# A bias copied into PSUM by ScalarE in place of a bias product, and other segment sizes, in a graph convolution kernel

## Chip, cores and metric

The kernel runs on one core of a Trainium2 chip. The metric is device time in microseconds, the median of several runs. A profile is one further execution of the same program, recorded by the hardware profiler.

## The reference

412,500 edges, sorted by their target node, join 12,500 nodes; each node and each filter has 128 features, each edge has 20 attributes.

```python
h    = maximum(layernorm(x), 0) @ W_in2f
Wij  = (ssp(edge_attr @ W_f1 + b_f1) @ W_f2 + b_f2) * edge_weight[:, None]   # ssp = softplus - log 2
x_ij = h[dst] * Wij                          # dst is sorted
agg  = segment_sum(x_ij, src, num_segments=12500)
out  = x + ssp(agg @ W_o1 + b_o1) @ W_o2 + b_o2
```

The rows of h are gathered by the sorted index, and the messages are summed by the unsorted one, so the sum is a scatter.

## The kernel before, in words

Edges are worked on in chunks of 512 (806 chunks; 4 chunks are a group, 202 groups). A chunk is four columns of 128 edges, one edge on each partition. Two things happen at once: messages are made and scattered into tables in DRAM, and tables that are full are read back and summed.

**Making messages.** The function `step(k)` writes out by hand the order of the work, so each engine's queue holds it in this order, whatever is ready first. For chunk k it does, among other things:

- `hidden` (lines 611 to 621), every second step for two chunks: two products `z` (line 616, TensorE), then Abs and Exp on ScalarE (lines 619 and 620). `hidden_log` is the Ln (line 625, in the other step), and `hidden_end` (line 631, VectorE) makes `r`.
- `value(k+1)` (lines 723 to 732): a product of three rows of ones with three bf16 parts of the bias starts the accumulation of `v` in a PSUM bank (line 726, 512 columns), and four fp32 products `r @ W_f2` (line 730) add to it.
- `picked(k+1)` (lines 711 to 721): four products gather the rows of h (line 714), and four ScalarE copies scaled by the edge weight make `hg` (line 719).
- `message(k)` (lines 734 to 757): VectorE multiplies `v` by `hg` into `o` (line 741), and GpSimd issues four indirect DMAs, one for each 128 edges, that scatter the rows of `o` (with the node's place as a 129th number) to slots of a table (line 745).
- `rank` and `rank_end` (lines 642 to 683): two products on a PSUM bank that is kept throughout (lines 687 and 655) and a VectorE maximum (line 660) find the next free slot of each node block. `blocks` and `window` are comparisons on VectorE (lines 636 and 706).

`v` and `picked` share three PSUM banks (tag "v", bufs=3); `o` has four buffers of two chunks each.

**Summing.** The groups are cut into segments, each with a table of its own: `SEGS = (64, 56, 32, 24, 14, 12)`. Each table has T tiles of 128 rows for each of the 98 node blocks, and one more for blocks near the segment's own nodes; T is 12, 11, 7, 5, 3 and 3. When a segment's chunks have been scattered, its table is read back in units of up to six tiles (`Collect.load`, line 783), VectorE compares the places with a row of numbers (line 794), and each tile is one fp32 product into `acc` (line 807), which is added to the sums in SBUF (line 822 or 824). A planner at lines 917 to 932 spreads the units of the first five segments evenly over the steps from nine after the segment's last chunk to step `NCH + 6` (NCH is 806): 5.39 tiles a step from step 265 to 489, 8.16 to step 713, and 8.24 after it. The last segment can only be collected when all its scatters have landed: it is a tail after the loop (lines 970 to 977), in which each four node blocks are finished at once by `finish` (lines 375 to 403: two more products, softplus, and the output). In tiles that is 4156 for all segments, 304 of them in the tail.

At the beginning, `make_h` (lines 299 to 362) computes h, partly beside the first steps.

Of the kernel before, what the change touches and what calls it, by code (L numbers as in the profile page):

```python
# [9 lines left out]
F32 = mybir.dt.float32  # L10
# [3 lines left out]
AF = mybir.ActivationFunctionType  # L14
# [3 lines left out]
P = 128  # L18
TG = 16
CH = 512  # L20
NCHUNK = TG * P // CH
QT = CH // P
SEGS = (64, 56, 32, 24, 14, 12)
RW = P + 1
VIEWS = 16
BG = 8
# [9 lines left out]
def ceil_div(a, b):  # L36
    return -(-a // b)
# [3 lines left out]
def gnn_kernel(  # L41
# [20 lines left out]
    nc = tc.nc  # L62
# [9 lines left out]
    const = ctx.enter_context(tc.tile_pool(name="const", bufs=1))  # L72

    NBLK = NTILE
    NFLAG = 6 * len(SEGS) + 8
    QB = QT * NBLK
    assert sum(SEGS) == NG
    NCH = ceil_div(n_edges, CH)

    class Segment:  # L80
# [4 lines left out]
        def __init__(self, k):  # L85
            self.g0 = sum(SEGS[:k])
            self.c0 = self.g0 * NCHUNK
            self.c1 = min((self.g0 + SEGS[k]) * NCHUNK, NCH)
            own = [c * CH * N // n_edges for c in (self.c0, self.c1)]

            self.b0 = max(0, own[0] - P // 2) // (P * BG) * BG
            self.b1 = min(NBLK, ceil_div(own[1] + P // 2, P * BG) * BG)
            mean = (SEGS[k] * TG * P - (own[1] - own[0])) / QT * P / N
            self.T = int(ceil_div(2 * (2 * mean + 4 * (2 * mean) ** 0.5), P))

            def low(m):
                return max(0, int(m - 5 * m ** 0.5)) // ZR * ZR

            self.low = low(mean)
            self.low_last = low(mean * (N % P or P) / P)  # L100
            self.rows = self.row(NBLK)
            self.table = tc.dram_tile([self.rows, RW], F32, name=f"slots{k}")

            self.views = dram_disjoint_views(self.table[:, :], VIEWS + 1)

            self.clears = []
            self.cleared = self.c0 + (self.c1 - self.c0) // 2 if k == 0 else self.c0
# [70 lines left out]
    def load(ap, shape, name):  # L178
        t = const.tile(shape, F32, name=name)
        nc.sync.dma_start(t, ap)  # L180
        return t
# [10 lines left out]
    wf2 = load(w_f2, [P, P], "wf2")  # L192
    wo1 = load(w_o1, [P, P], "wo1")
    wo2 = load(w_o2, [P, P], "wo2")
    bf1 = load(b_f1[:, None], [P, 1], "bf1")
    bo1 = load(b_o1[:, None], [P, 1], "bo1")
    bf2 = load(b_f2[None, :].to_broadcast([P, P]), [P, P], "bf2")
# [6 lines left out]
    def spread(t, n):  # L204
        return t[:, None, :].to_broadcast([t.shape[0], n, P])
# [24 lines left out]
    ones_b = const.tile([P, P], BF16, name="ones_b")  # L230
# [8 lines left out]
    nbf1 = const.tile([P, 1], F32, name="nbf1")  # L239
    nc.vector.tensor_scalar(nbf1, bf1, -1.0, None, op0=ALU.mult)  # L240

    bf2_p = const.tile([3, P], BF16, name="bf2_p")
    left = const.tile([1, P], F32, name="bf2_left")
    with tc.tile_pool(name="bias_ps", bufs=1, space=PSUM) as bias_ps:
        b12 = bias_ps.tile([1, P], F32, name="b12")
        nc.tensor.matmul(b12, bf1, wf2, start=True, stop=True)
        nc.vector.tensor_add(left, b12, bf2[0:1, :])
    for k in range(3):
        part = const.tile([1, P], BF16, name=f"bf2_{k}")
        nc.vector.tensor_copy(part, left)  # L250
# [7 lines left out]
    sums = tc.dram_tile([SUMT * P, P], F32, name="sums")  # L258
    segs = [Segment(k) for k in range(len(SEGS))]

# [225 lines left out]
    with tc.tile_pool(name="edge", bufs=2) as edge, tc.tile_pool(  # L486
        name="quad", bufs=3
# [44 lines left out]
        class Group:  # L532
# [176 lines left out]
            def picked(self, c, at):  # L709

                ps = psum.tile([P, QT, P], F32, name="picked", tag="v", bufs=3)
                near = self.near.pop(c)
                for i in range(QT):
                    nc.tensor.matmul(ps[:, i, :], at[:, i * P:(i + 1) * P], near,  # L714
                                     start=True, stop=True)
                hg = quad.tile([P, QT, P], F32, name="hg", bufs=2)
                for i in range(QT):
                    j = c * QT + i
                    nc.scalar.activation(hg[:, i, :], ps[:, i, :], AF.Copy,  # L719
                                         scale=self.rcut[:, j:j + 1])  # L720
                return hg

            def value(self, c):

                v = psum.tile([P, QT, P], F32, name="v", bufs=3)
                nc.tensor.matmul(v.rearrange("p t f -> p (t f)"), ones_b[:3, :], spread(bf2_p, QT),  # L726
                                 start=True, stop=False, skip_group_check=True)
                r = self.pair[c // 2 * 2][:, c % 2, :]
                for i in range(QT):
                    nc.tensor.matmul(v[:, i, :], r[:, i * P:(i + 1) * P], wf2,  # L730
                                     start=False, stop=True, skip_group_check=True)
                return v
# [98 lines left out]
        def of(k):  # L831
            return groups[k // NCHUNK], k % NCHUNK

        hgs, ats, vs = {}, {}, {}

        summed = []

        def step(k, units=()):


            def has(j):
                return 0 <= j < NCH

            j = k + LG
            if has(j) and j % NCHUNK == 0:
                groups[j // NCHUNK] = Group(j // NCHUNK)
            if has(k + LW):
                g, c = of(k + LW)
                g.rows(c)
            for c, u in units:  # L850
                c.load(u + AHEAD)

            j = k + LR + 1
            if has(j):
                g, c = of(j)
                if c == 0:
                    g.columns()
                g.blocks(c)
            j = k + LZ - 2
            if has(j) and j % 2 == 0:  # L860
                g, c = of(j)
                g.hidden_end(c)
            if has(k + 2):
                g, c = of(k + 2)
                g.window(c)
                ats[k + 2] = g.pick
            if has(k):
                g, c = of(k)
                g.message(c, vs.pop(k), hgs.pop(k))
            if has(k + 1):  # L870
                g, c = of(k + 1)
                vs[k + 1] = g.value(c)
            if has(k + 1):
                g, c = of(k + 1)
                hgs[k + 1] = g.picked(c, ats.pop(k + 1))
            for c, u in units:
                c.compare(u)
            j = k + LR
            if has(j):
                g, c = of(j)  # L880
                g.rank(c)
            j = k + LZ
            if has(j) and j % 2 == 0:
                g, c = of(j)
                g.hidden(c)
            j = k + LZ - 1
            if has(j) and j % 2 == 0:
                g, c = of(j)
                g.hidden_log(c)
            for c, u in units:  # L890
                if summed:
                    summed[0].add(summed[1])
                summed[:] = c, u
            j = k + LR
            if has(j):
                g, c = of(j)
                g.rank_end(c)
# [18 lines left out]

        at = [seg.c1 + 9 for seg in segs[:-1]]
        work = [sum(seg.tiles(b) for b in range(NBLK)) for seg in segs[:-1]]
        end = NCH + 6
        rate = {}  # L920
        while len(rate) < len(at):
            n = len(at) - len(rate)
# [3 lines left out]
            end = at[j]  # L926
# [22 lines left out]
        with tc.manual_schedule():  # L949
            h = [make_h(q, psum) for q in range(2)]  # L950
            for m in h + h:
                next(m)
            aside = side()
            relative()
            while h:
                for m in list(h):
                    if next(m, 1):
                        h.remove(m)
            for k in range(-LG, max(NCH, max(units) + 1)):
                for seg, d in zeros.get(k, ()):  # L960
                    seg.clears.append(nc.sync.dma_start(*d).ins.name)
                now = units.get(k, ())
                for c, u in now:
                    if u == 0:
                        for i in range(AHEAD):
                            c.load(i)
                step(k, now)
                next(aside, None)
            summed[0].add(summed[1])
# [13 lines left out]
    with tc.If(missed > 0):  # L983
        with tc.tile_pool(name="any_e", bufs=2) as edge, tc.tile_pool(
            name="any_q", bufs=2
# [51 lines left out]
```

## Time and profile before

| | |
|---|---|
| median of 3 runs | 5830.78 us (5822.29 to 5839.35) |
| the profiled execution | 4396.31 us, its span 4394.5 us |
| mean granted TensorE clock in it | 0.855 of full speed |
| busy: TensorE products, VectorE, GpSimd, ScalarE | 3607, 3140, 3115, 2333 us |
| the 16 DMA engines | mean 189 GB/s |

The profiled execution was 1434 us shorter than the median of the timed runs. So durations of single instructions can be read from the profile, and sums over it are to be held against its own time; what the timed runs did otherwise isn't on the page.

In the rows, a group is named by its line, engine and operation; an fp32 product is recorded as two instructions, so the 4156 tiles of line 807 are 8312 rows. The clock column says which part of full speed TensorE was granted. Of an engine's idle time the profile says what ended it.

### The profile page before, as it was taken

The numbers are of one execution on the slowest core, as the hardware profiler recorded it, in microseconds if no ns is written. First come the engines' busy times: TensorE is split into PE (matmuls) and PEld (weight loads), VectorE is DVE, ScalarE is ACT, GpSimd is POOL, SyncE is SP. The second block draws the span as 40 slices with busy tenths as digits, with TensorE's granted clock in tenths as the row PEclk, the third lists the DMA queues.
The fourth block names the chain that finished last, engine by engine and source line by source line (L and its number), as shares of the span: only waits on it lengthen the run. The fifth ranks groups of instructions, "written<-read, shape, count | busy, mean of one in ns | idle before, by whom it ended". The sixth has DMA issues, their size and how long they took to land.

```text
span 4394.5 us, 72656 instructions
## 1 busy us (share of the span) xinstructions
PE 3607.4 (82%) x22558; PEld 2618.3 (60%) x22558; DVE 3140.1 (71%) x6637; ACT 2332.5 (53%) x4685; POOL 3114.6 (71%) x3288
## 2 busy tenths in 40 slices
PE   3767776777777888888788889999899998989877
PEld 2544444444444666666566567777677776767666
DVE  5766666566555776767667678787888878888766
ACT  3655555555555555555555555555555555545424
POOL 2777777677777777777777777777777777777620
PEclk9776666667666898899998899999999999999999
DMA  5766547888765666765876566666666766766666
GB/s 139 192 178 230 174 128 197 223 223 230 183 208 135 177 178 183 238 193 166 257 197 174 150 179 187 194 195 185 189 188 183 199 191 185 193 188 191 172 180 192
DMA packets 498071, 829.10 MB, mean 189 GB/s; under 512 B 170680, under 2 KB 288300, under 8 KB 497676
## 3 DMA queue, kind: packets, MB, share of 16 engines
q1 hardware_dynamic: 378950, 602.34, 51.2%
q0 software_dynamic: 103168, 213.15, 14.7%
q10 hardware_dynamic: 15558, 8.89, 0.7%
q8 instruction: 182, 2.98, 0.3%
q14 instruction: 213, 1.74, 0.1%
HBM read 425.03 MB, written 398.98 MB: 188 GB/s over the span
## 4 chain that ended last, share of the span: by engine, by line


## 5 line engine op out<-in xcount | busy, mean ns | idle before, releaser
L745 POOL DMA_INDIRECT slots<-o,slot x3224 | 3108.4, 964 | 1106.3 <-issue 803.6
L719 ACT ACTIVATE hg<-picked,rcut 128x128 f32<-128x128 f32 x3224 | 920.8, 369 | 1372.0 <-PE picked L714 1323.5
L807 PEld LDWEIGHTS acc<-to,m 128*128 128x128 f32 x8312 | 1078.7, 205 | 353.8 <-issue 187.7
L807 PE MATMUL acc<-to,m 128*128 128x128 f32 x8312 | 1154.6, 294 | 92.3 <-DVE agg L824 47.3
L730 PEld LDWEIGHTS v<-wf,r 128*128 128x128 f32 x6448 | 918.1, 220 | 303.7 <-issue 303.7
L730 PE MATMUL v<-wf,r 128*128 128x128 f32 x6448 | 1088.2, 320 | 0.0
L616 PE MATMUL z<-f,wf 20*128 20x512 f32 x1612 | 524.2, 726 | 217.5 <-DVE r L631 190.9
L794 DVE TENSOR_TENSOR to<-count_ps,m 128x768 f32<-128x768 f32 (+3 forms) x829 | 657.9, 812 | 51.8 <-PE acc L807 27.7
L619 ACT ACTIVATE a<-z,bf 128x1024 f32<-128x1024 f32 x403 | 449.1, 1114 | 426.7 <-PE z L616 426.7
L660 DVE TENSOR_REDUCE top<-free 128x4 f32<-128x392 f32 x806 | 447.2, 555 | 211.7 <-PE free L655 210.4
L631 DVE SCALAR_TENSOR_TENSOR r<-z,nbf,a 128x1024 f32<-128x1024 f32 x403 | 514.6, 1277 | 94.2 <-ACT a L625 92.5
L741 DVE TENSOR_TENSOR o<-v,hg 128x512 f32<-128x512 f32 x806 | 547.2, 679 | 2.8 <-ACT hg L719 2.1
L739 DVE COPY o<-place 128x8 f32<-128x8 f32 x403 | 80.4, 200 | 650.9 <-DMA slots<-o,slot 650.6
L714 PE MATMUL picked<-near,at 96*128 96x128 bf16 x3224 | 356.4, 240 | 218.0 <-DVE o L741 215.7
L625 ACT ACTIVATE a<-a,half 128x1024 f32<-128x1024 f32 x403 | 468.4, 1162 | 0.0
L636 DVE TENSOR_TENSOR inb<-count_ps,blk 128x392 f16<-128x392 f32 x806 | 445.7, 553 | 0.0
L726 PE MATMUL v<-bf_p,ones_b 3*128 3x512 bf16 x806 | 350.1, 434 | 104.1 <-DVE o L741 93.9
L620 ACT ACTIVATE a<-a 128x1024 f32<-128x1024 f32 x403 | 425.9, 1057 | 12.8
L714 PEld LDWEIGHTS <-at 96*128 96x128 bf16 x3224 | 275.7, 109 | 256.2 <-DVE o L741 224.6
L616 PEld LDWEIGHTS z<-f,wf 20*128 20x128 f32 x1612 | 142.4, 206 | 388.9 <-issue 186.3
L687 PE MATMUL free<-inb,rest_of 128*128 128x392 f16 x806 | 303.1, 376 | 55.0 <-DVE top L660 53.8
L706 DVE TENSOR_TENSOR at<-rel,prow 96x512 bf16<-96x512 bf16 x806 | 331.1, 411 | 0.0
(107 smaller groups left out, 1416.2 us busy)
## 6 DMA issues: line engine op xcount, KB each, us to landing
m<-slots SPq DMA_DIRECT2D x371, 387.0 KB
rel<-rel_d SPq DMA_DIRECT2D x202, 384.0 KB
m<-slots SPq DMA_DIRECT2D x172, 322.5 KB
m<-slots SPq DMA_DIRECT2D x212, 258.0 KB
slots<-o,slot POOLq DMA_INDIRECT x3224
slots<-zero SPq DMA_DIRECT2D x24, 2064.0 KB
f<-in_f_t SPq DMA_DIRECT2D x404, 80.0 KB
slots<-zero SPq DMA_DIRECT2D x22, 1032.0 KB
```

The source lines that it names most:

```text
L616: nc.tensor.matmul(z[:, k, :], wf1[rows, :], self.f[rows, :], start=True, stop=True)
L619: nc.scalar.activation(a, z, AF.Abs, bias=bf1)
L625: nc.scalar.activation(a, a, AF.Ln, bias=half, scale=0.5)
L631: nc.vector.scalar_tensor_tensor(r, z, nbf1, a, op0=ALU.max, op1=ALU.add)
L660: nc.vector.tensor_reduce(self.top[:, c * QT:(c + 1) * QT], free_v, axis=mybir.AxisListType.X, op=ALU.max)
L714: nc.tensor.matmul(ps[:, i, :], at[:, i * P:(i + 1) * P], near, start=True, stop=True)
L719: nc.scalar.activation(hg[:, i, :], ps[:, i, :], AF.Copy, scale=self.rcut[:, j:j + 1])
L730: nc.tensor.matmul(v[:, i, :], r[:, i * P:(i + 1) * P], wf2, start=False, stop=True, skip_group_check=True)
L741: nc.vector.tensor_mul(o[:, :, :P], v, hg)
L745: put = nc.gpsimd.indirect_dma_start(out=views[j % VIEWS], out_offset=bass.IndirectOffsetOnAxis(ap=self.slot[:, j:j + 1], axis=0), in_=o[: ...
L794: nc.vector.tensor_tensor(to[:, :n, :], count_ps[:, None, :].to_broadcast([P, n, P]), self.m[u][:, :n, P:].to_broadcast([P, n, P]), op=ALU ...
L807: nc.tensor.matmul(self.acc[b // QT][:, i, :], m[:, j, :P], to[:, j, :], start=t == 0, stop=t == self.seg.tiles(b) - 1)
```

## The change

Two things are changed. The bias row, which is the same for every edge, is laid out over 128 partitions once, in a tile `bf12`. For every chunk from the third on, ScalarE copies it into the PSUM bank of `v` (`bias`), and the four products of `value` add to what they find there; the first two chunks keep the product. The copy for chunk k+2 is queued in step k, behind the four `hg` copies of chunk k+1 and ahead of Abs, Exp or Ln. The `picked` products set their start flag once for a bank and not four times. And the segments are of 64, 56, 36, 24, 14 and 8 groups, with the planner's end at `NCH + 14`; T becomes 12, 11, 7, 5, 3 and 2, which makes 4058 tiles, 206 of them in the tail.

```diff
-SEGS = (64, 56, 32, 24, 14, 12)
+SEGS = (64, 56, 36, 24, 14, 8)
...
+    bf12 = const.tile([P, P], F32, name="bf12")
...
-        b12 = bias_ps.tile([1, P], F32, name="b12")
-        nc.tensor.matmul(b12, bf1, wf2, start=True, stop=True)
-        nc.vector.tensor_add(left, b12, bf2[0:1, :])
+        b12 = bias_ps.tile([P, P], F32, name="b12")
+        nc.tensor.matmul(b12, bf1.to_broadcast([P, P]), wf2, start=True, stop=True)
+        nc.vector.tensor_add(bf12, b12, bf2)
+    nc.vector.tensor_copy(left, bf12[0:1, :])
...
                     nc.tensor.matmul(ps[:, i, :], at[:, i * P:(i + 1) * P], near,
-                                     start=True, stop=True)
+                                     start=i == 0, stop=i == QT - 1, skip_group_check=True)
...
-            def value(self, c):
+            def bias(self, c):
                 v = psum.tile([P, QT, P], F32, name="v", bufs=3)
-                nc.tensor.matmul(v.rearrange("p t f -> p (t f)"), ones_b[:3, :], spread(bf2_p, QT),
-                                 start=True, stop=False, skip_group_check=True)
+                if self.g * NCHUNK + c < 2:
+                    nc.tensor.matmul(v.rearrange("p t f -> p (t f)"), ones_b[:3, :],
+                                     spread(bf2_p, QT), start=True, stop=False,
+                                     skip_group_check=True)
+                else:
+                    nc.scalar.activation(v, spread(bf12, QT), AF.Copy)
+                return v
+
+            def value(self, c, v):
                 r = self.pair[c // 2 * 2][:, c % 2, :]
...
-                vs[k + 1] = g.value(c)
-            if has(k + 1):
-                g, c = of(k + 1)
+                vs[k + 1] = g.value(c, bs.pop(k + 1))
                 hgs[k + 1] = g.picked(c, ats.pop(k + 1))
+            if has(k + 2):
+                g, c = of(k + 2)
+                bs[k + 2] = g.bias(c)
...
-        end = NCH + 6
+        end = NCH + 14
```

## The prediction, as put on record before the result

> **What bounds the kernel now.** I read the groups first, then the engines by stretch with the clock, then GpSimd's queue, then single steps in order of time. In the groups (line, engine, operation, tiles, count | busy us, mean ns | idle before it), these matter:
>
> ```profile
> L745 POOL DMA_INDIRECT slots<-o,slot x3224 | 3108.4, 964 | 1106.3 <-issue 803.6
> L807 PE MATMUL acc<-to,m 128*128 128x128 f32 x8312 | 1154.6, 294 | 92.3 <-DVE agg L824 47.3
> L739 DVE COPY o<-place 128x8 f32<-128x8 f32 x403 | 80.4, 200 | 650.9 <-DMA slots<-o,slot 650.6
> L726 PE MATMUL v<-bf_p,ones_b 3*128 3x512 bf16 x806 | 350.1, 434 | 104.1 <-DVE o L741 93.9
> L822 ACT ACTIVATE agg<-acc 128x512 f32<-128x512 f32 x24 | 14.2, 591 | 3.4 <-PE acc L807 3.4
> ```
>
> The page puts GpSimd at 71% busy and TensorE at 82%, but VectorE waits 650.6 us for scatters to land so that it gets an `o` buffer back: whoever makes messages is ahead of who scatters them. GpSimd's queue, in order of time (start, duration):
>
> ```profile
> 2999.11 0.95 POOL L745 DMA_INDIRECT slots<-o,slot  x1 [0.31 <-DVE to L794]
> 3000.37 0.96 POOL L745 DMA_INDIRECT slots<-o,slot  x1 [0.30 <-issue]
> 3001.63 0.96 POOL L745 DMA_INDIRECT slots<-o,slot  x1 [0.30 <-issue]
> ```
>
> Start to start is 1.26 us, so a chunk of four takes 5.05 us. By stretch (the columns are length; busy us and instructions of PE, weight load, DVE, ACT, POOL; clock; DMA share; GB/s):
>
> ```profile
> 400.00:600.00 200.00, 145.75 (x737) 89.73 (x737) 128.23 (x317) 117.59 (x244) 152.14 (x158) 0.71 0.57 176
> 3000.00:3200.00 200.00, 182.36 (x1316) 142.81 (x1316) 164.08 (x320) 106.56 (x214) 151.83 (x159) 0.96 0.68 189
> 4220.00:4394.00 174.00, 132.88 (x930) 113.92 (x930) 113.62 (x165) 61.78 (x100) 1.28 (x2) 0.96 0.69 198
> ```
>
> 158 or 159 scatters fit in each 200 us, early and late. So the profiled execution is bound by GpSimd: about 84 us before the first scatter, 3224 × 1.265 = 4078, some stalls, and a tail of 174 us add up to its 4394.5 us. But the timed runs take 5830.78 us, 1434 us more, and this page doesn't say why. It has a hint: the granted clock is often 0.50 while TensorE is busy without a gap. From one such place (start, duration):
>
> ```profile
> 1183.55 0.63 PE L714 MATMUL picked<-near,at 96*128 96x128 bf16 x4
> 1183.98 0.53 PE L687 MATMUL free<-inb,rest_of 128*128 128x392 f16 x1
> 1184.30 0.53 PE L655 MATMUL free<-inb,after 128*128 128x392 f16 x1
> 1184.77 2.08 PE L616 MATMUL z<-f,wf 20*128 20x512 f32 x4
> 1186.63 0.63 PE L726 MATMUL v<-bf_p,ones_b 3*128 3x512 bf16 x1
> 1187.19 2.08 PE L730 MATMUL v<-wf,r 128*128 128x128 f32 x8
> 1189.06 0.63 PE L714 MATMUL picked<-near,at 96*128 96x128 bf16 x4
> 1189.49 0.53 PE L687 MATMUL free<-inb,rest_of 128*128 128x392 f16 x1
> 1189.82 0.53 PE L655 MATMUL free<-inb,after 128*128 128x392 f16 x1
> 1190.93 0.58 PE L726 MATMUL v<-bf_p,ones_b 3*128 3x512 bf16 x1 [0.58 <-ACT hg L719]
> ```
>
> The clock there (length, busy us, count, clock, DMA share, GB/s):
>
> ```profile
> 1180.00:1185.00 5.00, 5.00 (x24) 0.50 0.66 149
> ```
>
> From start to start at half clock: bias product 0.53 to 0.56 us, the four products of v 1.87, picked 0.43, the two rank products 0.8, a pair of z 1.87. A step with z is 5.48 us (1181.15, the bias product before the first line shown, to 1186.63) and one without 3.66 of work, 4.57 on average. A tile of line 807 is two instructions like those of v: 1.87 / 4 = 0.47 us. Now suppose that the timed runs have half clock throughout, and TensorE binds wherever a step of it takes over 5.05 us:
>
> - 80 us of start, and 265 steps before any segment is collected: the pair of steps takes 9.78 us with its wait for hg (1181.15 to 1190.93), 4.89 a step, with about 0.25 of make_h 5.14: 1362.
> - 224 steps with 5.39 tiles: 4.57 + 2.52 = 7.09 each: 1588. 224 with 8.16: 8.38 each: 1877. 93 with 8.24: 8.42 each: 783. Six more: 23.
> - Tail: 304 tiles × 0.47 = 142, and 25 times 3.7 for the two output products (two runs of 1.87): 235 in all.
>
> The sum is 5948 us, 2% over the median and with nothing fitted to it. GpSimd's rate would have to become 1.7 us for no reason that the trace shows. I take it that the timed runs are TensorE at about half clock.
>
> **What the Trainium skill says.** "TensorE: Matmul & The Clock Gate", section "Part 1: The HAM clock gate", has two clock states only, half and full, with half as the default; the trace agrees in its plain 0.50 and 1.00. The page also says that some 3.4 us of activity release it. The trace doesn't agree: from 1005 to 1020 us TensorE was 89 to 100% busy at 0.50. That keeps my reading possible, and doesn't prove it. "Perfetto Trace Analysis", section "GPSIMD Engine Instruction", advises start-to-start spacing over recorded spans, hence 1.26 and not 0.96 us. "ScalarE: Activation LUTs", section "What ACT_TABLE_LOAD costs", prices an ACTIVATE with immediate scale and bias at 186 ns + 0.833 ns an element: an estimate of 613 ns for the new copy. The trace's nearest row, L822, took 591 ns. "PSUM — Partial Sum Buffer", section "The four PSUM rules", says that a product without a start flag adds to what ScalarE wrote only where an earlier product left its mark; that is why picked's flags change, which costs nothing: same products.
>
> **The change, part by part.**
>
> - Removed: 804 bias products, 0.53 us each at half clock (0.31 at full: 3000.46 to 3000.77), and their weight loads, which overlap.
> - Added: 804 copies on ScalarE at 0.59 us = 474 us, onto 2333 of busy time. Both ends: 0.37 (an hg copy, a quarter of the size) and 0.72 (L372). ScalarE then has 2807 us of work in over 5400; it doesn't bind.
> - The new wait: v's first product needs the copy, which stands behind the hg of the chunk before it. From picked's end it is ready after about 0.05 + 1.14 (four hg) + 0.59 + 0.1 = 1.9 us. Behind the waiting product in TensorE's queue are picked, the rank products, z and acc; for hg, message and then GpSimd wait. Cover in a step: two rank products 0.8, z 1.87 every second step, and one or two units of acc, 1.9 us (4 tiles) to 2.8 (6 tiles). With a unit the wait is hidden; planned rates give about one unit in every step from step 265. Without a unit or z, 1.1 us show; the old product too waited 0.58 there. Queued behind the copy are Abs, Exp or Ln, 0.6 us later; z's banks and r have a step of slack.
> - Early stage (265 steps): with z 5.48 − 0.53 = 4.95, without it 1.87 + 0.43 + 1.95 = 4.25; 4.6 on average, with make_h 4.85. That is under GpSimd's 5.05: 1338 instead of 1362. So 265 of the savings are cut to 24 us.
> - Later stages, 0.53 less a step, with the new plan: 224 × 6.56 = 1469; 240 steps with 7.62 tiles × 7.60 = 1824; 77 with 8.97 × 8.23 = 634; 14 steps of 4.19 = 59.
> - Tail: 206 tiles × 0.47 + 93 = 189. The segments' part of the saving is 98 tiles × 0.47 = 46 us. Fewer rows are cleared and read back as well, beside other work.
> - Setting up bf12: one larger product and one more small copy, under 1 us before the first scatter, and hidden by the loads.
>
> The sum after is 80 + 1338 + 1469 + 1824 + 634 + 59 + 189 = 5593, so 355 less. Scaled by 5831 / 5948 it is 348: **5830 − 348 = 5482, say 5480 us.** In the profiled execution, where GpSimd binds, the same edit should give only the shorter tail: 98 tiles at 0.25 us (1.0 / 4 at full clock), some 25 us off 4396.
>
> **Rivals.**
>
> - *A: GpSimd binds in the timed runs too*, at some 1.7 us a scatter. For it: it does bind in the profile. Against: no row shows such a rate. Then only the tail gives: 5830 − 25 to 30 = 5803, at the edge of what can be told.
> - *B: the copy is late, and TensorE waits for it (slower).* Place: ScalarE's queue, where picked may end while Abs and Exp (2.2 us) still run. Then the copy comes after 4.1 us, and a step with rank and one small unit (2.5 of cover) waits 1.6; in half the steps that is 0.8 a step against 0.53 saved. Over 541 steps +146, less 46 for the tiles: 5930. It decides from a mean wait of about 0.6 us a step. Against it: ScalarE is 53% busy and waits 1323.5 us for picked.
> - *C: the clock state isn't a property of the runs but of the kernel*, and the new order falls into full clock: 4396 − 25 = 4370.
>
> **Chances and range.** Forecast 0.60 (own range 5390 to 5570: no early saving, or waits of 0.15 a step, at one end; the unscaled sum and a copy of 0.37 at the other), A 0.18, B 0.17, C 0.05. The range 5390 to 5860 takes in the forecast, A and the near end of B. Faster by over 0.3% (what a measurement here can tell): 0.60 + 0.12 of A + 0.05; same 0.06; slower 0.17.
>
> **What would show it.** The timed median falls by some 6% while the profiled execution falls by under 1%. Line 726 is left with two products; a copy of 128x512 at about 0.6 us appears 804 times; v's first product waits for ScalarE mostly before the first collection. If the profile still shows 158 scatters in 200 us and the median hardly moves, A is right; if v waits for the copy in stretches with acc, B is. The forecast is wrong at its root if a timed run isn't at half clock.

## The result, and the profile after

The changed kernel took **5878.36 us** (median of 8 runs, 5857.70 to 5899.12), the kernel before beside it 5826.53 us (8 runs). The ratio is 1.0091, interval 1.0061 to 1.0120: slower by 0.9%. The forecast was 5480 us and its range ended at 5860. The profiled execution took 5886.37 us, its span 5884.6 us at a clock of 0.747; the eight runs have 0.747 to 0.753.

One thing has to be known to read the pages: the kernel before takes about 4390 us at some times and 5800 to 5880 us at others. The page of before came from the first kind, its timed runs and everything of after from the second; so these two pages can't be held against each other line by line. The experiments and the result give times of both kinds for both kernels. The experiments were run in six groups, each on another chip at another hour, so chip and hour weren't parted: where the text speaks of a kind of chip, it may as well be a condition of the hour.

The groups of after that answer to those shown of before (line, engine, operation, tiles, count | busy us, mean ns | idle before it, what ended it), from the page and the list of groups:

```profile
L757 POOL DMA_INDIRECT slots<-o,slot x3224 | 3103.2, 963 | 2591.0 <-DVE o L753 1671.5
L742 PE MATMUL v<-wf,r 128*128 128x128 f32 x6448 | 1235.5, 352 | 1460.6 <-ACT v L735 1120.9
L722 ACT ACTIVATE hg<-picked,rcut 128x128 f32<-128x128 f32 x3224 | 920.8, 368 | 2387.2 <-remote 1437.7
...
L819 PE MATMUL acc<-to,m 128*128 128x128 f32 x8116 | 1298.5, 316 | 316.8 <-issue 155.3
...
L735 ACT ACTIVATE v<-bf 128x512 f32<-128x512 f32 x804 | 489.4, 609 | 17.6 <-DVE at L708 2.3
```

A scatter itself takes as long as before (963 ns), but GpSimd now idles 2591 us, mostly for VectorE's messages. By stretch (length; busy us and instructions of PE, weight load, DVE, ACT, POOL; clock; DMA share; GB/s):

```profile
400.00:600.00 200.00, 111.49 (x530) 76.53 (x528) 99.26 (x249) 105.73 (x212) 118.07 (x123) 0.64 0.48 155
3000.00:3200.00 200.00, 125.33 (x778) 98.51 (x777) 104.32 (x207) 97.35 (x193) 113.48 (x118) 0.77 0.44 123
5700.00:5884.00 184.00, 136.25 (x923) 115.75 (x922) 119.20 (x185) 61.79 (x100) 0.96 (x1) 0.95 0.64 181
```

118 scatters fit in 200 us where it was 159, and no engine is busy for more than 63% of that stretch (159 is from the page of before). What lies between is seen in order of time (start, duration, and in brackets the idle time of the engine before it):

```profile
2966.00 0.39 PE L717 MATMUL picked<-near,at 96*128 96x128 bf16 x4
...
2968.54 0.82 PE L819 MATMUL acc<-to,m 128*128 128x128 f32 x5
...
2969.73 0.27 PE L819 MATMUL acc<-to,m 128*128 128x128 f32 x1 [0.36 <-issue]
...
2970.44 0.36 PE L819 MATMUL acc<-to,m 128*128 128x128 f32 x1 [0.45 <-issue]
...
2971.83 0.27 PE L819 MATMUL acc<-to,m 128*128 128x128 f32 x1 [1.03 <-issue]
...
2977.64 1.14 ACT L722 ACTIVATE hg<-picked,rcut 128x128 f32<-128x128 f32 x4 [11.62 <-remote]
2977.68 0.57 DVE L662 TENSOR_REDUCE top<-free 128x4 f32<-128x392 f32 x1 [8.47 <-remote]
```

TensorE waits for nothing that the profile shows ("issue"), yet starts its products only every 0.7 or 1.4 us, where five took 0.82 us just before. `picked` is recorded at 2966.4 as done, but `hg` starts 11 us later, together with VectorE's `top`, which also waits for TensorE. I call such a place a standstill. Counted in the traces as stretches of over 3 us in which ScalarE and VectorE are both idle, after has 223 of them, 1181 us in all, some 25 us apart; the profiled execution of before has 20 with 96 us, and the changed kernel at 4.4 ms (x5 below) 23 with 117 us.

### The profile page after: what moved, and what is told of

Its sections match the earlier page's. It is cut to its first block, busy times and chain, and to the rows that moved or that the text cites. A ratio compares the mean times of both kernels' runs of the same rounds, so it can differ in the third digit from the quotient of the medians.

```text
span 5884.6 us, 71400 instructions
## 1 busy us (share of the span) xinstructions
PE 3745.9 (64%) x21558; PEld 2872.0 (49%) x21558; DVE 3151.1 (54%) x6633; ACT 2775.0 (47%) x5489; POOL 3109.4 (53%) x3288
## 4 chain that ended last, share of the span: by engine, by line
## 5 line engine op out<-in xcount | busy, mean ns | idle before, releaser
L742 PE MATMUL v<-wf,r 128*128 128x128 f32 x6448 | 1235.5, 352 | 1460.6 <-ACT v L735 1120.9
L742 PEld LDWEIGHTS v<-wf,r 128*128 128x128 f32 x6448 | 1090.0, 255 | 1733.2 <-ACT v L735 1301.5
L819 PEld LDWEIGHTS acc<-to,m 128*128 128x128 f32 x8116 | 1196.0, 226 | 643.5 <-issue 414.3
L819 PE MATMUL acc<-to,m 128*128 128x128 f32 x8116 | 1298.5, 316 | 316.8 <-issue 155.3
L618 PE MATMUL z<-f,wf 20*128 20x512 f32 x1612 | 593.6, 805 | 181.1 <-DVE r L633 92.1
L735 ACT ACTIVATE v<-bf 128x512 f32<-128x512 f32 x804 | 489.4, 609 | 17.6 <-DVE at L708 2.3
L717 PE MATMUL picked<-near,at 96*128 96x128 bf16 x3224 | 400.0, 260 | 3.0 <-issue 2.9
L689 PE MATMUL free<-inb,rest_of 128*128 128x392 f16 x806 | 338.8, 420 | 49.7 <-DVE top L662 45.6
L657 PE MATMUL free<-inb,after 128*128 128x392 f16 x806 | 336.8, 418 | 7.1 <-DVE inb L638 2.9
L717 PEld LDWEIGHTS <-at 96*128 96x128 bf16 x3224 | 322.4, 121 | 29.9 <-issue 2.8
```

Of the source, the lines that this page charges most:

```text
L618: nc.tensor.matmul(z[:, k, :], wf1[rows, :], self.f[rows, :], start=True, stop=True)
L735: nc.scalar.activation(v, spread(bf12, QT), AF.Copy)
L742: nc.tensor.matmul(v[:, i, :], r[:, i * P:(i + 1) * P], wf2, start=False, stop=True, skip_group_check=True)
L819: nc.tensor.matmul(self.acc[b // QT][:, i, :], m[:, j, :P], to[:, j, :], start=t == 0, stop=t == self.seg.tiles(b) - 1)
```

## Experiments

Ratios are to the kernel before on the same chip in the same hour. Some runs leave a part of the result out: x4 and x17 the filter's bias, x6, x7 and x10 the messages of each chunk's fourth column.

| run | edit | before beside it | this | ratio (interval) |
|---|---|---|---|---|
| x1 | before as it is | 4391.03 | 4388.09 | 0.9991 (0.9977 to 1.0004) |
| x2 | copy alone | 4391.03 | 4378.35 | 0.9968 (0.9956 to 0.9980) |
| x3 | segments alone | 4391.03 | 4394.47 | 1.0008 (0.9999 to 1.0016) |
| x4 | no bias at all | 4391.03 | 4377.17 | 0.9968 (0.9956 to 0.9979) |
| x5 | the whole change | 4390.10 | 4371.87 | 0.9955 (0.9938 to 0.9971) |
| x6 | before, 3 of 4 scatters | 4390.10 | 4243.45 | 0.9660 (0.9639 to 0.9681) |
| x7 | after, 3 of 4 scatters | 4390.10 | 4187.13 | 0.9533 (0.9510 to 0.9555) |
| x8 | before with pauses | 5809.48 | 6218.82 | 1.0695 (1.0648 to 1.0743) |
| x9 | after with pauses | 5809.48 | 6257.00 | 1.0758 (1.0710 to 1.0806) |
| x10 | x7 with an early copy | 5809.48 | 5506.73 | 0.9466 (0.9425 to 0.9506) |
| x11 | copy alone | 4387.80 | 4375.60 | 0.9977 (0.9968 to 0.9986) |
| x12 | segments alone | 4387.80 | 4392.80 | 1.0012 (1.0003 to 1.0021) |
| x13 | after with an early copy | 4387.80 | 4774.97 | 1.0888 (1.0852 to 1.0923) |
| x14 | x13 with four banks | 4387.80 | 4691.67 | 1.0692 (1.0671 to 1.0714) |
| x15 | copy alone | 5879.70 | 5933.04 | 1.0077 (1.0050 to 1.0105) |
| x16 | segments alone | 5879.70 | 5858.20 | 0.9968 (0.9948 to 0.9987) |
| x17 | no bias at all | 5823.20 | 5799.09 | 0.9967 (0.9948 to 0.9986) |
| x18 | before with a copy nobody reads | 5823.20 | 5896.33 | 1.0127 (1.0092 to 1.0161) |

**Is it the clock? The kernel before again, and the two halves of the change (x1 to x4).** The copy alone is the diff with the old `SEGS` and `NCH + 6`; the segments alone are its first and last lines; x4 takes the product out:

```diff
-                nc.tensor.matmul(v.rearrange("p t f -> p (t f)"), ones_b[:3, :], spread(bf2_p, QT),
-                                 start=True, stop=False, skip_group_check=True)
...
-                                     start=False, stop=True, skip_group_check=True)
+                                     start=True, stop=True)
```

> The kernel before, unchanged, for a second profile at the time of its median. Theory P (the prediction's): TensorE at half clock binds; then the profile lies near 5830 us with a clock of about 0.5, TensorE over 90% busy, and hardly a wait of it. Theory H (formed on the trace after): between bursts of work TensorE's results reach ScalarE and VectorE several us late, some 200 times in a run; then the clock is about 0.75, TensorE about 65% busy, and there are some 200 gaps of over 3 us in which ScalarE and VectorE are both idle, summing to 1000 to 1300 us.

> The copy alone, with the old segments and the old planner's end. P: 804 products less, of which 541 bind: about 5830 - 300 = 5530. H: the copy lengthens the way from picked over hg to v by 0.6 us where the product took 0.3 to 0.5, so it costs rather than saves: 5860 to 5930.

> The segments and the planner's end alone, with the bias product. P: 98 tiles less at 0.47 us: 5785. H: the same tail at about full clock, 98 x 0.25, and the two output products: 25 to 50 less, 5780 to 5805. The two theories don't differ here; it gives this part's size.

> The kernel before with neither product nor copy: b_f2 (with its share of b_f1) is left out of the computation, and the four products of v start their own columns. P: as the copy, about 5530. H: only what the product takes in the chain, 0.3 to 0.5 us in a part of the chunks: 5600 to 5780, clearly below the copy alone by more than 100 us.

All four ran at 4371 to 4401 us, the profile of x1 with a clock of 0.846. Both theories had been put for 5800 us, so none of their numbers applies here. But the page of before was no oddity: on this chip, in that hour, its timed runs are like it. Taking the product out gains 0.3%, and with the copy in its place the gain is the same. The segments bring nothing.

**The whole change at 4.4 ms, and both kernels with GpSimd relieved (x5 to x7).** x6 and x7 issue three of a chunk's four scatters and clear all tables before the first step:

```diff
-                return max(0, int(m - 5 * m ** 0.5)) // ZR * ZR
+                return 0
...
-            self.cleared = self.c0 + (self.c1 - self.c0) // 2 if k == 0 else self.c0
+            self.cleared = self.c0
...
-                for i in range(QT):
+                for i in range(QT - 1):
...
-            zeros.setdefault(i * (seg.cleared - 20) // len(todo), []).append((seg, d))
+            zeros.setdefault(-LG, []).append((seg, d))
```

> The changed kernel as it is, on the chip of the runs before it. Theory G (GpSimd's stream of scatters sets the pace at 1.26 us each, and the 5,800 us runs come from a condition in which this chip is not): about 4,380 us, that is the sum of copy alone (-13 us) and segments alone (+3 us), ratio 0.995 to 1.000. Theory W (the +0.9% of the result is a wait that the change adds and that any run of it has): 4,391 * 1.009 = 4,430 us or more. If the run shows long stretches in which ScalarE and VectorE stand still together, and the kernel before shows none beside it, the stalls belong to the change and not to the chip.

> The kernel before with GpSimd relieved: three of the four scatters of a chunk are issued (the fourth column's messages are left out of the sums), and all tables are cleared before the first step, which delays the start. Theory G: GpSimd needs 3 * 1.265 * 806 = 3,059 us in place of 4,078, so another engine becomes the bound. TensorE had 3,646 us of work in the unchanged kernel, VectorE 3,141; the steady part should come to 3,650 to 3,950 us, plus the later start, and TensorE's share of busy time should rise from 83% to about 90%. Theory W (a chain of hand-overs picked, hg, product, bank sets the pace, about 5 us a chunk): no shorter than 4,300 us.

> The changed kernel with the same relief as its neighbour (a quarter of the scatters left out, all clears first). It shows what the copy is worth when GpSimd does not hold it. If TensorE's work binds there: less by 806 times the bias product's issue of 0.29 us at full clock to 0.47 at half, that is 230 to 350 us below its neighbour. If the chain of hand-overs binds (hg of a step, then the copy on ScalarE, then the bank for v): no gain, or up to 0.3 us a chunk (240 us) more than its neighbour. Between the two, a gain under 100 us says that the copy's wait gives back most of what the product took.

Here the change gains 0.45%. Its trace, by group and by stretch:

```profile
L757 POOL DMA_INDIRECT slots<-o,slot x3224 | 3115.3, 966 | 1087.7 <-issue 795.3
L722 ACT ACTIVATE hg<-picked,rcut 128x128 f32<-128x128 f32 x3224 | 917.7, 367 | 937.2 <-PE picked L717 896.2
```

```profile
3000.00:3200.00 200.00, 166.31 (x1233) 136.22 (x1232) 156.29 (x301) 129.26 (x254) 152.12 (x158) 0.95 0.65 180
```

158 scatters in 200 us again. I worked out the spacing of all scatters from both traces of the changed kernel: the median is 1.263 us in both, but spacings over 1.5 us are 42 in x5, which cost 33 us over the normal one, and 418 in the profile of after, which cost 1532 us. The difference, 1499 us, is that of the spans but for 11 (5884.6 − 4374.4 = 1510). So the two kinds differ in how often GpSimd is left without messages, not in how fast it is. Nor are the transfers slower: a packet of the DMA engines took 93 ns on average in both traces.

In x6 the first scatter starts at 352 us in place of 84, and from it to the last are 3724 us, within the 3650 to 3950 that theory G gave; so GpSimd's pace did bind, and theory W falls. With GpSimd relieved the change gains more, 4243.45 − 4187.13 = 56 us. TensorE's busy time fell by 354 us (3450.4 to 3096.6), 340 of them the bias products; its idle time rose by 292 us, and 276 us are booked as waits of v for the copy, which x6 doesn't have. From the waits of x7 (us in total, times, longest):

```profile
POOL slots L757 <- DVE o L753: 665.6, 383, 11.9
ACT hg L722 <- PE picked L717: 575.5, 619, 6.8
...
PE v L742 <- ACT v L735: 276.0, 210, 9.7
```

**Pauses written into both kernels, and the copy ahead of hg (x8 to x10).** The pause (EVERY is 6, which makes 135 pauses; late_d is a strip in DRAM), and the order in `step` in x10:

```diff
+                if "hg" in kept and (self.g * NCHUNK + c) % EVERY == 0:
+                    late = edge.tile([P, P], F32, name="late")
+                    rows = slice(32 * c, 32 * c + RBF)
+                    nc.scalar.dma_start(late_d, kept["hg"][:RBF, QT - 1, :])
+                    nc.scalar.dma_start(late[rows, :], late_d)
+                    nc.tensor.matmul(z[:, 0, 0:1], late[rows, :], late[rows, 0:1],
+                                     start=True, stop=True)
```

```diff
+            if has(k + 2):
+                g, c = of(k + 2)
+                bs[k + 2] = g.bias(c)
+            if has(k + 1):
+                g, c = of(k + 1)
                 hgs[k + 1] = g.picked(c, ats.pop(k + 1))
-            if has(k + 2):
-                g, c = of(k + 2)
-                bs[k + 2] = g.bias(c)
```

> The kernel before with a pause written into it: at every sixth chunk a product of one column on TensorE (overwritten by the next product, so that the result is the same) waits for a strip of hg that ScalarE's queue stores to memory and loads back, which should hold TensorE some 4 to 6 us, 135 times, with ScalarE and VectorE running dry behind it. It imitates, by other means, the standstills that the trace of the changed kernel's own session shows about every 25 us. Expected 4,700 to 5,200 us: 135 pauses of 5 us are 675 us on top of TensorE's 3,646 us of work and its waits.

> The changed kernel with the same pauses. Theory S (after a pause the copy stands behind the late hg on ScalarE, and v's first product behind the copy, so each restart is longer by about a copy, 0.6 us): 135 * 0.6 = 80 us, less what the missing product gives back, thus about as long as its neighbour or up to 2% longer, as in the result. Theory T (TensorE has less work and catches up sooner): 100 to 350 us shorter than its neighbour; then the result's +0.9% is not what pauses of TensorE alone do to this change.

> The changed kernel with a quarter of the scatters left out and all clears first, as before, and with the copy for step k+2 issued ahead of picked and hg of step k+1 in place of behind them. If the copy's place behind hg on ScalarE is what gives back the gain (waits of v for the copy of 276 + 465 us there), these waits fall by more than half, and the ratio to the kernel before falls from 0.953 to 0.93 or less. If another engine's work or the bank binds, the ratio stays within 0.95 to 0.96 and the wait shows up at another line (picked for VectorE's product).

They came onto a chip of the 5.8 ms kind, which has standstills of its own; so the pauses imitate nothing there, and the numbers expected for x8 don't apply (the pauses cost 409 us, 3.0 us each). What remains is a second measurement of the change, though in kernels with pauses: x9 over x8 is 1.0758 / 1.0695 = 1.006, near the result. x10 can't be compared with x7, which ran on the other kind; the wait of v for the copy did go, and picked's wait for VectorE's product (1233.9 us) came instead.

**The early copy where GpSimd binds (x11 to x14).** x13 is after with the order of x10. x14 adds:

```diff
-        count_ps = state_ps.tile([P, P], F32, name="count_ps")
-        nc.scalar.activation(count_ps, places, AF.Copy)
+        count_ps = places
...
-                ps = psum.tile([P, QT, P], F32, name="picked", tag="v", bufs=3)
+                ps = psum.tile([P, QT, P], F32, name="picked", tag="v", bufs=4)
...
-                v = psum.tile([P, QT, P], F32, name="v", bufs=3)
+                v = psum.tile([P, QT, P], F32, name="v", bufs=4)
```

> The copy alone, old segments, once more, to have it also on a chip where the kernel before takes 5,800 us. Where it takes 4,390 us: ratio 0.997 again. Where it takes 5,800: theory S (the copy stands behind hg, hg behind a late picked, and v's products behind the copy) expects that the loss of the result is here, ratio 1.005 to 1.012; its rival (the loss comes from the segments, and the missing product gains as it does elsewhere) expects 0.97 to 1.000.

> The segments and the later end of the sums alone, with the bias product. Where the kernel before takes 4,390 us: 1.0008 again. Where it takes 5,800: theory S expects 0.997 to 1.003; the rival expects 1.005 to 1.012.

> The changed kernel with the copy for step k+2 issued ahead of picked and hg of step k+1. Where the kernel before takes 4,390 us GpSimd binds: ratio 0.993 to 1.000, as without it. Where it takes 5,800: theory S expects the wait of v for the copy (1,121 us on TensorE after the change) to fall to under 400 us and the ratio from 1.009 to between 0.94 and 0.99; picked will wait for VectorE's product instead (1,234 us in the run with a quarter of the scatters left out), which can give all of it back, and then the ratio stays at 0.99 to 1.01.

> The same early copy with four banks for v and picked in place of three; the bank comes from the row of place numbers, which VectorE's comparisons then read from SBUF and not from PSUM. If the waits for a bank are what the early copy pays with, picked's wait for VectorE falls to under 300 us and, where the kernel before takes 5,800 us, the ratio falls below that of x13_early by 0.01 or more. Where it takes 4,390 us: GpSimd binds, 0.993 to 1.003.

x11 and x12 repeat x2 and x3. For x13 I expected that GpSimd would hide the new order, and it became 8.9% slower. Its waits:

```profile
ACT hg L722 <- PE picked L717: 1504.7, 629, 8.4
PEld L717 <- DVE o L753: 1046.5, 436, 5.7
PE picked L717 <- DVE o L753: 985.1, 444, 5.6
...
PE v L742 <- ACT v L735: 8.5, 10, 1.0
```

I read it so: the copy takes the free bank first, and picked has to wait until VectorE has read the bank of v; product, picked, hg and the next product then stand in one ring with little overlap. With four banks (x14) that wait falls to 374 us, which fits (under 300 was expected), but the run stays slow for another reason:

```profile
L756 POOL DMA_INDIRECT slots<-o,slot x3224 | 3460.7, 1073 | 1079.6 <-issue 811.5
```

A scatter takes 1073 ns in place of 966; 3224 × 0.107 = 345 us, which is more than the 304 us lost. In x14 VectorE's comparisons read both operands from SBUF. Scatters that overlap the comparison `to` take 1.25 us on average there, the others 1.01 (0.97 for both in x13), and those that overlap neither `to` nor `inb`, the other comparison that was moved, 0.98. The Trainium skill, "SBUF — State Buffer", section "SBUF: two separate sides", says that a VectorE operation with two SBUF inputs and a GpSimd operation that reads SBUF lock each other out of a shared pair of ports; the trace agrees in direction. Whether a scatter counts as such a read is not shown, and the fourth bank alone wasn't tried.

**The two halves of the change where the kernel takes 5.8 ms (x15, x16).** The kernels are those of x2 and x3.

> The copy alone, for the third time. Where the kernel before takes 4,390 us: 0.997 as before. Where it takes 5,800 us: theory S (the copy waits behind a late hg, and v behind the copy) 1.005 to 1.012; its rival (the segments make the loss) 0.97 to 1.000.

> The segments alone, for the third time. Where the kernel before takes 4,390 us: 1.000 to 1.002 as before. Where it takes 5,800 us: theory S 0.997 to 1.003; its rival 1.005 to 1.012.

The copy makes the loss (1.0077), and the segments give 0.3% back. Together that is 1.0045, half of the result's 1.0091, which was measured on its own, at another hour; the intervals still overlap. The waits in x15:

```profile
ACT hg L722 <- remote: 1375.0, 203, 13.2
...
PE v L742 <- ACT v L735: 1195.1, 260, 16.0
```

and in x16, which has the product:

```profile
ACT hg L719 <- remote: 1432.9, 213, 14.2
...
PE v L726 <- ACT hg L719: 339.8, 81, 10.4
...
PE picked L714 <- ACT hg L719: 279.2, 67, 12.8
```

This looked like theory S, by which the loss is v's wait for the copy: it is 1195 us. But x16, without the copy, has over 600 us of such waits at other places. A wait that contains a standstill is booked on whichever instruction comes next.

**The copy's work without its wait (x17, x18).** x17 is the kernel of x4, x18 the kernel before with

```diff
+        unread = state.tile([P, QT, P], F32, name="unread")
...
+            if has(k + 2):
+                nc.scalar.activation(unread, spread(places, QT), AF.Copy)
```

after picked and hg in `step`.

> Neither the product nor the copy (b_f2's term is left out), once more. Where the kernel before takes 4,390 us: 0.997 again. Where it takes 5,800 us: theory S (the loss is the wait for the copy, and TensorE's freed 0.48 us a step is worth something there) expects 0.96 to 0.99, since TensorE, at 71% busy, stands at the head of each late hand-over. If the ratio is within 0.995 to 1.005 the freed time is worth nothing there either, and the copy's wait costs its 0.8% from zero.

> The kernel before, with its products, and a copy of the same size on ScalarE in the place where the changed kernel has it, into a buffer that nothing reads. Where the kernel before takes 4,390 us: 1.000 to 1.003, since ScalarE goes from 53% to 64% busy with room left. Where it takes 5,800 us: theory S (the wait of v counts, not ScalarE's work) expects 0.998 to 1.004; its rival (the copy delays the next Abs, Ln or hg on ScalarE) 1.006 to 1.02.

Theory S isn't needed. A copy that nobody waits for costs 1.27%, so the copy's work is enough; taking the product out gives 0.33%. The sum, +0.94%, is what the copy in its place cost (+0.77%) within the intervals: v's new wait adds nothing that can be told, where half a per cent could hide. The two copies aren't quite alike: the one of x18 writes to SBUF, takes 648 ns in place of 609, and needs no bank. How ScalarE can matter when it is 46% busy shows in the trace of x18 after a standstill:

```profile
3027.30 1.14 ACT L720 ACTIVATE hg<-picked,rcut 128x128 f32<-128x128 f32 x4 [9.71 <-PE acc L808]
...
3028.32 0.65 ACT L878 ACTIVATE unread<-places 128x512 f32<-128x512 f32 x1
...
3028.84 1.13 ACT L620 ACTIVATE a<-z,bf 128x1024 f32<-128x1024 f32 x1
...
3030.00 1.06 ACT L621 ACTIVATE a<-a 128x1024 f32<-128x1024 f32 x1
...
3032.56 0.64 ACT L878 ACTIVATE unread<-places 128x512 f32<-128x512 f32 x1
3033.08 1.16 ACT L626 ACTIVATE a<-a,half 128x1024 f32<-128x1024 f32 x1
...
3034.28 1.28 DVE L632 SCALAR_TENSOR_TENSOR r<-z,nbf,a 128x1024 f32<-128x1024 f32 x1 [0.42 <-issue]
```

For 7 us ScalarE has hardly a gap, and VectorE's `r`, which frees the banks of z, comes behind two copies. Over all standstills ScalarE is the busiest engine in the first 3 us after them: 80% in x16, 89% in x18 (TensorE 53 and 52%), and in the next 3 us 41 and 59%. 73 us over 199 standstills is 0.37 us each, about half a copy. That the copy costs is shown; that it costs at these places is a reading of the trace, which no run parted.

## Why the prediction was wrong

- **"I take it that the timed runs are TensorE at about half clock"** is the step that failed, and the saving of 348 us with it. The timed runs of after have a clock of 0.747 to 0.753, and those of the kernel before itself, beside x8, x15 and x17, 0.734 to 0.753. TensorE is busy 64% of the span of after and 71% in x16, which keeps the product, and every engine has gaps. The sum of 5948 us agreed with the median within 2% with nothing fitted, and was still a coincidence. What the runs show in its place are holes in GpSimd's stream: 1532 us in the profile of after (1511 in x16), where the page of before has 48. Some 1100 of the 1532 us lie at a standstill (they touch one, or follow it within 3 us); where the rest comes from is open, and the kernel before itself has no profile at 5.8 ms. I had taken the missing cause to be one that the page hinted at, when it wasn't on the page.
- **"GpSimd's rate would have to become 1.7 us for no reason that the trace shows"** was the argument against rival A. The mean spacing did become (5700.1 − 86.1) / 3223 = 1.74 us, as 1.26 us with 418 holes. A mean rate can change without any instruction being longer. Rival A isn't right all the same: GpSimd is 53% busy there and waits for messages, so it doesn't bind.
- **The saving of 0.53 us a step** exists in part as work: 340 us less of bias products from x6 to x7, 0.42 us each. It is worth nothing like that: 56 us with GpSimd relieved, 0.3% on either kind of chip when only the product is taken out (x4, x17).
- **The copy's price** was right, 0.59 us against 0.609 and 0.606 measured; the estimate of 613 ns from the Trainium skill, "ScalarE: Activation LUTs", section "What ACT_TABLE_LOAD costs", too. That ScalarE "doesn't bind" was argued from its mean share, and it was wrong on the 5.8 ms chips: with the product gone the copies cost 0.8% there (x15), and beside the product 1.3% (x18).
- **The cover** ("with a unit the wait is hidden") was too hopeful: in x7 v waits 276 us for the copy, 0.34 us a step.
- **The tail.** "Some 25 us off 4396" on the profiled kind of chip: x5 has 18 us. But that it is near is luck, since few of them come from the tail: from the last scatter to the end it is 168 us in x1 and 166 in x5, for other segments' units have moved into it (684 rows of `acc` there before, 595 after; I had counted 608 and 412). In the traces most come from fewer holes in GpSimd's stream (47 us over the normal spacing in x1, 33 in x5), and the halves say the same: the copy alone gives 12 to 13 us, the segments alone cost 3 to 5.
- **Rival B** (slower, 5930 us by a late copy that TensorE waits for) had the sign, at twice the size (100 us for the measured 52), and in x15 a wait of 1.5 us a step is booked, well over its deciding 0.6. That is luck in the main, since its mechanism isn't needed: x18 has the cost without the wait.
- **Rival C**'s number, 4370 us, came up in x5 (4371.87), by luck too: the kernel before took 4390 beside it, at nearly the same clock.
- **The own range.** Its lower end, 5390, doesn't follow from the sums shown: the unscaled saving gives 5831 − 355 = 5476.
- **Not settled:** what makes TensorE start one instruction in 0.7 us, some 200 times in a run of one kind and hardly at all in the other. No edit here was shown to turn it on or off. In x10 there are few such standstills (45 in all; the 43 from the first scatter on make 157 us), but its steps still took longer than those of x13, which has the same order at 4.4 ms: 4955 us from the first scatter to the last against 4513. So the standstills as counted aren't the whole of the difference. The number of instruction fetches is the same in both traces of the changed kernel (175 and 216 packets on their two queues), so more of them isn't the cause; whether they are slow to arrive, or the number of records matters, wasn't tried.

## What to carry to other kernels

When a profiled execution and the timed runs differ by a quarter, no change should be priced until a run shows which condition the timed ones are in; a sum that happens to meet the median doesn't show it. An engine at 45% of the span may still be the one that everybody waits for just after a stall, so work moved onto it is to be priced there, and a copy that nobody reads prices it without the new wait. And where two tiles share a few banks, moving one allocation earlier changes who waits for whose bank: follow the ring before moving it.

## What the runs showed of the hardware

- One program took 4388 to 4391 us in three groups of runs and 5809 to 5880 us in three others (medians of the kernel before, each group on another chip at another hour), steady within about 1% in each, with clocks of 0.82 to 0.86 and 0.73 to 0.75.
- In the second kind ScalarE sees TensorE's results late: from the end of picked, as recorded, to hg on an idle ScalarE is never over 3 us in x5, and over 3 us 224 times in the profile of after, some 1690 us in all. Whether the hand-over is late or TensorE ends later than its records say, the trace doesn't tell. The hand-over from VectorE to GpSimd, where GpSimd stood idle, has a median of 0.28 us in x6 and x7 as in the profile of after.
- In x14 a comparison on VectorE with both operands in SBUF goes with longer scatters on GpSimd: 1.25 us against 1.01 (a fourth bank was added in the same run).
- A ScalarE copy of 128x512 takes 598 to 609 ns from SBUF to PSUM, and 648 ns from SBUF to SBUF.
